# Batch 1's first FFN half prepared and begun before the first exponentials of batch 0's attention

## The chip, the cores and the metric

The kernel runs on one core of a Trainium2 chip. The metric is the device time of one execution in microseconds (us). Before the change it is 2087.34 us, the median of 3 runs (2084.44 to 2087.61).

## The reference

The input x is (4, 1024, 256) in float32: 4 batches of 1024 rows. Three steps follow one another, each added to x:

```python
x = x + 0.5 * ffn(layernorm(x))       # mixture of 8 experts, 2 chosen per row, and a shared one
x = x + attn_block(layernorm(x))      # 16 heads of 64, then an MLP of 256 -> 512 -> 256
x = x + 0.5 * ffn(layernorm(x))       # the same weights again
```

In the FFN a router (a 256 x 8 product, a sigmoid, the two largest scores, divided by their sum) gives each row a weight for every expert. Each expert is `gelu(x @ W1 + b1) @ W2 + b2` with 128 hidden values and the exact GELU. The shared expert has the same sizes and no weight. In the attention, scores are divided by 16 and a mask adds -999 to one corner element of the 1024 x 1024 scores (first query, last key); then softmax, values, output projection, and an MLP with the tanh form of GELU.

## The kernel before, in words

All large products are made of three float16 matmuls: each operand is split in a high and a low half (`mm3`, L952), and the products high-high, high-low and low-high are added in PSUM.

**Attention** runs over 32 pairs of heads (4 batches x 8 pairs), each in 4 units (2 heads x 2 halves of the queries), each unit in 4 steps: 512 steps, numbered i. Three things belong to a step. `maxima` (L1405) multiplies a block of 128 queries by all keys (two matmuls at L1425) into the PSUM tile S0, and DVE reduces it (L1432). After four of them a short chain, `row` (L1456), writes the negative maxima into the operand `low` by a DMA (L1467). `scores` (L1470) makes 2 x 512 transposed scores with the maxima already subtracted, four matmuls (L1489, L1490) into S1; ACT takes the exponential (line L550, in the helper `tabled`), ACT casts it to float16 (L1501), and POOL subtracts for the low half (L1504). `values` (L1525) multiplies by V. Maxima run LM = 6 steps ahead of scores.

**Jobs.** FFN and MLP work is done in halves of a batch (512 rows), each a `Job`. An FFN job (`ffn`, L1056) has `prep` (layer norm by `stats`, transposing by `transposed`, the router, and the loads of three gate rows `gb`), nine first layers (`layer`, L1101, six matmuls each at the helper line L948, then `rest`: GELU on ACT, times the gate on DVE at L1138, a cast on ACT at L1148, a subtraction on DVE at L1153), and four `second` parts (27 matmuls with W2 and one with the biases). The shared expert is number 8 and goes first in `ORDER`; it has no gate and one DVE step (L1151). Batch 0's two jobs (`fronts[0]`) run first, in `first_jobs` (L391), before attention; there the gate is made by a matmul (L1121) in one of four half tiles of S0 and S1, called places. All later jobs run between attention's steps.

**The order is planned by hand.** `Order` (L100) keeps a model clock for PE, ACT, DVE and POOL. Each piece of work is a generator, a chain with a rank, that yields `Ask`s: engine time, a PSUM bank (`BANK`; three F banks), an `ld` buffer (`LD`; two), a condition (`IF`), or a time to land (`DMA`). `until` (L269) waits in the model for the next step of attention and lets chains use PE meanwhile (`other`); `share` (L286) gives chains `SHARE` us of PE before and after each step's scores. `choose` (L217) lets a chain's operation go ahead of attention's own on an engine only if it ends at most a little late. Instructions of those four engines go to the chip in the planned order. SP, which issues all DMAs, is in order as well, but its order is not written out here.

GELU and the exponential use different ACT tables. `gelus` counts GELUs that are owed. While it is above zero, no exponential is planned: `exps` carries the condition

```python
self.then("ACT", 1.03, exps, 0, lambda: self.pt_live < BPT and self.order.gelus == 0)
```

`serve` (L429) takes the jobs after batch 0 in turn, and `prepare` (L381) runs the prep of the next one. In the kernel before, both wait until batch 0's two jobs are done entirely, and the nine layers of an FFN job are made together by `block` (L1626), which stops the exponentials, takes S0 and S1 too, and puts layer after layer on PE. A job starts only when the PE time given to jobs is below `target`, `RATE * (max(i, 0) + NEAR) + DONE`.

`attention` (L1574) starts with `ahead(14)`, which waits for `low_ready`, then for the first projections, and issues the first stack (`stack`, L1346: DMAs that lay Q and K of a head as `AC` and `low`). Seven maxima come before the first score.

Of the kernel before, what the change touches and what calls it, by code (L numbers as in the profile page):

```python
# [51 lines left out]
RANK, RREST = -2, -3  # L52
WAIT, AGE, LATE, LPOOL, SLOW = 2.0, 0.2, 1.6, 2.3, 0.7
SHARE, RATE, LEAD, NEAR, OWED = 0.7, 0.58, 40, 20, -16.0
BLD = 2
# [21 lines left out]
GBT, ROWT, MWT = 4.2, 3.2, 8.0  # L77
DONE = 23.4
NV = 3
LM = 6  # L80
# [225 lines left out]
class Kernel:  # L306
# [74 lines left out]
    def prepare(self):  # L381

        while True:
            yield Ask("IF", lambda: self.fronts[0][1].done and self.prep_ok and all(j.done for j in self.ends) and bool(self.jobs) and
                      not self.jobs[0].prepared and (self.jobs[0].dep is None or self.jobs[0].dep.done))
            job = self.jobs[0]
            for ask in job.prep:
                yield ask
            job.prepared = True

    def first_jobs(self):  # L391
# [4 lines left out]
        order.places = [(0.0, h) for h in self.halves]  # L396
        self.passed, self.exps = [False, False], 0

        def job(n, job):
# [14 lines left out]
            self.passed[n] = True  # L414
            yield Ask("IF", lambda: job.evicts == 0)
            order.start(self.ending(job), -8)

        self.setup()
        for n, j in enumerate((one, two)):
            order.start(job(n, j), -12 + n)  # L420

    def place_for(self, to):
# [6 lines left out]
    def serve(self, job, hp):  # L429

        yield Ask("IF", lambda: all(j.done for j in self.fronts[0]))
        while True:
            if job is None:
                yield Ask("IF", lambda: not self.closing and bool(self.jobs) and self.jobs[0].prepared and
                          self.order.done[3] < self.target)
                job = self.current = self.jobs.pop(0)
                self.prep_ok = False
                raw, hp = self.hidden(False)
                if job.pieces > 4:
                    self.block = job, hp  # L440
                    yield Ask("IF", lambda: self.block is None)
                else:
                    yield from job.burst(raw, hp)
                    yield Ask("IF", lambda: job.left == 0)
                self.prep_ok = True
# [513 lines left out]
    def router(self, xt, slot, half, spread):  # L959

        nc, wk = self.nc, self.mp
        n = 4
        own, at = spread and self.order is not None, []
        if own:
# [60 lines left out]
        elif not spread:  # L1025
            self.free()
            yield Ask("BANK")
            yield Ask("LD", 1)
        yield Ask("PE", 0.44)
# [21 lines left out]
        elif not spread:  # L1051
            self.free()
            self.free_ld()
        return gt

    def ffn(self, x, slot, half, burst, after, dep=None):  # L1056
# [44 lines left out]
        def layer(i, e, hp, ps, free=None):  # L1101
# [6 lines left out]
            def rest():  # L1108
                own, at = spread and self.order is not None, []
                if own and e < E:  # L1110
# [50 lines left out]
        def second(t, hp):  # L1161
            own, at = spread and self.order is not None, []
            if own:
# [87 lines left out]
    def front_h(self, b, half, x=None):  # L1251
# [12 lines left out]
        for t in range(4):  # L1264
            yield Ask("POOL", 0.56)
            nc.gpsimd.tensor_scalar(h[:, t, :], x[:, t, :], r[:, t, 0:1], nb[:, t, 0:1], ALU.mult, ALU.add)
        yield Ask("IF", lambda: self.bo_ready)
        for t in range(4):
# [305 lines left out]
    def attention(self):  # L1574
# [11 lines left out]
        def ahead(i):  # L1586
# [7 lines left out]
            if i == 14:  # L1594
                order.until(lambda: self.low_ready or None, 0)
            for lead, part in ((14, 0), (17, 1)):
# [66 lines left out]
        with self.tc.manual_schedule(engines={E_.PE, E_.Activation, E_.DVE, E_.Pool}):  # L1663
            self.first_jobs()
            order.start(self.serve(None, None), 3, 4.0)
            order.start(self.prepare(), 4)
            for i in range(-A, N + LVX):
                self.target = RATE * (max(i, 0) + NEAR) + DONE
# [219 lines left out]
```

## Time and profile before

| | us |
|---|---|
| median of 3 runs | 2087.34 |
| profiled execution, time | 2090.07 |
| its span | 2088.3 |
| first exponential starts | 140.3 |
| last exponential starts | 1931.2 |
| PE busy | 1975.2 |
| DVE busy | 1468.7 |
| ACT busy | 1496.9 |
| POOL busy | 1400.3 |

The span runs from the first to the last instruction of the profiled execution. Of it 140 us lie before the first exponential (weights split, batch 0's FFN, first projections), 1791 us are attention with the jobs between its steps, and 157 us are the last MLP and FFN halves. In the answers below, an instruction's line is followed by engine, operation, output <- input, shape and count, and in brackets by the idle time of its engine just before it and what ended that. SPq is the queue of DMA issues. Window rows give for each engine the busy us and, in brackets, the count.

### The profile page before, as it was taken

The numbers are of one execution on the slowest core, as the hardware profiler recorded it, in microseconds if no ns is written. First come the engines' busy times: TensorE is split into PE (matmuls) and PEld (weight loads), VectorE is DVE, ScalarE is ACT, GpSimd is POOL, SyncE is SP. The second block draws the span as 40 slices with busy tenths as digits, with TensorE's granted clock in tenths as the row PEclk, the third lists the DMA queues.
The fourth block names the chain that finished last, engine by engine and source line by source line (L and its number), as shares of the span: only waits on it lengthen the run. The fifth ranks groups of instructions, "written<-read, shape, count | busy, mean of one in ns | idle before, by whom it ended". The sixth has DMA issues, their size and how long they took to land.

```text
span 2088.3 us, 53062 instructions
## 1 busy us (share of the span) xinstructions
PE 1975.2 (95%) x22468; PEld 1287.9 (62%) x22468; DVE 1468.7 (70%) x2460; ACT 1496.9 (72%) x1785; POOL 1400.3 (67%) x891
## 2 busy tenths in 40 slices
PE   6979999999999999999999999999999999989789
PEld 3635666665666666657566666666665666656456
DVE  6567776766777777776777767677677576765654
ACT  6347768678777787778777768787778587777653
POOL 6654848577766987748577877777576788776300
PEclk9989999999999999999999999999999999999899
DMA  6532322434332423144324231333222414231100
GB/s 177 151 80 80 100 80 57 120 80 106 74 90 67 97 52 92 48 107 87 95 60 125 69 85 50 95 74 85 69 70 77 110 34 105 43 91 37 31 1 31
DMA packets 213020, 166.22 MB, mean 80 GB/s; under 512 B 140991, under 2 KB 172872, under 8 KB 212782
## 3 DMA queue, kind: packets, MB, share of 16 engines
q1 hardware_dynamic: 212782, 162.83, 30.9%
q8 instruction: 176, 2.88, 0.6%
q14 instruction: 62, 0.51, 0.1%
HBM read 70.18 MB, written 13.83 MB: 40 GB/s over the span
## 4 chain that ended last, share of the span: by engine, by line
PE 78%; ACT 5%; issue 3%; POOL 3%; DVE 2%; DMA 1%; POOLq 0%; ACTq 0%; DVEq 0%; SPq 0%
PE F L948 30%; PE S L1489 10%; PE S L1490 9%; PE S L1425 9%; PE av L1542 6%; PE av L1541 5%; PE av L1539 5%; POOL pk L1504 2%; ACT pt L550 2%; PE S L948 1%; ACT pk L1501 1%; ACT L550 1%; PE S L1459 1%; ACT ld L897 0%; DMA hp<-mwd 0%
## 5 line engine op out<-in xcount | busy, mean ns | idle before, releaser
L1504 POOL TENSOR_TENSOR pk<-pt,pk 128x1024 f16<-128x1024 f32 x512 | 1088.4, 2133 | 428.2 <-ACT pk L1501 208.2
L1432 DVE TENSOR_REDUCE mx<-S 128x1 f32<-128x1024 f32 x512 | 626.1, 1223 | 287.8 <-PE S L1425 262.0
L550 ACT ACTIVATE pt<-S 128x1024 f32<-128x1024 f32 x512 | 524.5, 1024 | 344.3 <-PE S L1490 321.0
L1501 ACT CAST pk<-pt 128x1024 f16<-128x1024 f32 x512 | 535.1, 1046 | 15.3
L1542 PE MATMUL av<-V,pk 128*128 128x65 f16 x4096 | 429.2, 193 | 16.9 <-POOL pk L1504 15.4
L1541 PE MATMUL av<-V,pk 128*128 128x64 f16 x4096 | 435.5, 195 | 0.0
L1539 PE MATMUL av<-V,pk 128*128 128x65 f16 x4096 | 434.6, 193 | 0.9 <-DVE at L1555 0.7
L1539 PEld LDWEIGHTS <-pk 128*128 128x128 f16 x4096 | 382.5, 97 | 54.4 <-issue 0.6
L1541 PEld LDWEIGHTS <-pk 128*128 128x128 f16 x4096 | 380.9, 97 | 53.9 <-issue 1.4
L1489 PE MATMUL S<-low 128*128 128x512 f16 x1024 | 389.6, 380 | 11.6 <-ACT pt L550 10.9
L1542 PEld LDWEIGHTS <-pk 128*128 128x128 f16 x4096 | 380.5, 99 | 22.3 <-POOL pk L1504 20.8
L1490 PE MATMUL S<-AC 128*128 128x512 f16 x1024 | 389.9, 381 | 0.0
L1425 PE MATMUL S<-AC 128*128 128x512 f16 x1024 | 307.6, 382 | 27.4 <-DVE mrow L1463 18.1
L948 PEld LDWEIGHTS <-hp 128*128 128x128 f16 x2100 | 206.1, 99 | 76.3 <-issue 9.3
L948 PE MATMUL F<-xA,wq 128*128 128x512 f16 x768 | 185.5, 379 | 1.1 <-DVE hp L1153 1.1
L948 PE MATMUL F<-wfs,hp 128*128 128x256 f16 x1404 | 180.4, 276 | 3.8 <-ACT u L550 2.8
L1490 PEld LDWEIGHTS <-AC 128*128 128x128 f16 x1024 | 100.1, 98 | 124.6 <-issue 37.3
L1489 PEld LDWEIGHTS <-low 128*128 128x128 f16 x1024 | 100.2, 98 | 106.4 <-issue 2.1
L948 PEld LDWEIGHTS <-wfs 128*128 128x128 f16 x864 | 84.1, 100 | 107.0 <-issue 17.6
L948 PEld LDWEIGHTS <-wq 128*128 128x128 f16 x768 | 74.3, 98 | 87.8 <-issue 1.9
L948 PE MATMUL F<-xF,wfs 128*128 128x512 f16 x504 | 122.9, 389 | 4.2 <-ACT u L550 2.8
L1425 PEld LDWEIGHTS <-AC 128*128 128x128 f16 x1024 | 75.4, 97 | 47.1 <-issue 33.5
(238 smaller groups left out, 2527.7 us busy)
## 6 DMA issues: line engine op xcount, KB each, us to landing
AC<-qk SPq DMA_DIRECT2D x128, 256.0 KB
gb<-gd SPq DMA_DIRECT2D x88, 256.0 KB
low<-qk SPq DMA_DIRECT2D x64, 256.0 KB
wq<-wqd SPq DMA_DIRECT2D x33, 384.0 KB
hp<-mwd SPq DMA_DIRECT2D x6, 1024.0 KB
x<-in_L_attn_x_dram SPq DMA_DIRECT2D x8, 512.0 KB
x1d<-x SPq DMA_DIRECT2D x8, 512.0 KB
wo<-wod SPq DMA_DIRECT2D x16, 256.0 KB
```

What stands on the lines that cost most here:

```text
L550: i = self.nc.scalar.activation(out, in_, func, **kw).ins
L948: i = self.nc.tensor.matmul(*args, start=start, **kw).ins
L1425: mm(ps[:, hs], AC[:, 0, qs], AC[:, 1, hs], start=True, stop=(h == 0 or t > 0), skip_group_check=True)
L1432: nc.vector.tensor_reduce(self.mx[:, t % 4:t % 4 + 1], ps, AX.X, ALU.max, negate=True)
L1459: nc.tensor.transpose(tp[:4, :P], mx[:], self.ident[:])
L1489: mm(o, low[:, 1, ks], low[:, 0, qs], start=True, stop=False, skip_group_check=True)
L1490: mm(o, AC[:, 1, ks], AC[:, 0, qs], start=False, stop=True, skip_group_check=True)
L1501: nc.scalar.copy(pk[:, 0], pt[:])
L1504: nc.gpsimd.tensor_tensor(pk[:, 1], pt[:], pk[:, 0], ALU.subtract)
L1539: mm(o[:, 0:65], pk[:, 0, ps], v[:, 0:65], start=(n == 0 and c == 0 and t == 0), stop=False, skip_group_check=True)
L1541: mm(o[:, 0:64], pk[:, 0, ps], v[:, 65:129], start=False, stop=False, skip_group_check=True)
L1542: mm(o[:, 0:65], pk[:, 1, ps], v[:, 0:65], start=False, stop=(n == 3 and c == 1), skip_group_check=True)
```

## The change

A new chain, `early_prep`, with rank `EARLY` = -6, runs the prep of batch 1's first half as soon as batch 0's first half has its `h` (`h_made`), that is while batch 0's second half runs. `prepare` starts after it (`early`), no longer after batch 0's jobs. `serve` starts when the last product of batch 0's second half is evicted (`over`). It makes the nine layers of its first job one by one in F banks, as chains that go where PE is free, and not as a block; GELUs are owed from that moment on. The router of that job uses places of S0 and S1 instead of F banks, and `ahead(14)` waits until it is through (`routed`). `SHARE` goes from 0.70 to 0.72.

```diff
-SHARE, RATE, LEAD, NEAR, OWED = 0.7, 0.58, 40, 20, -16.0
+SHARE, RATE, LEAD, NEAR, OWED = 0.72, 0.58, 40, 20, -16.0
+EARLY = -6
 def prepare(self):
-            yield Ask("IF", lambda: self.fronts[0][1].done and self.prep_ok and all(j.done for j in self.ends) and bool(self.jobs) and
+            yield Ask("IF", lambda: self.early and self.prep_ok and all(j.done for j in self.ends) and bool(self.jobs) and
...
 def first_jobs(self):
-        self.passed, self.exps = [False, False], 0
+        self.passed, self.exps, self.h_made, self.over = [False, False], 0, False, False
+        self.early = self.routed = False
...
             yield Ask("IF", lambda: job.evicts == 0)
+            self.over = n == 1
             order.start(self.ending(job), -8)
+    def early_prep(self):
+
+        yield Ask("IF", lambda: self.h_made)
+        for ask in self.jobs[0].prep:
+            yield ask
+        self.jobs[0].prepared = self.early = True
 def serve(self, job, hp):
-        yield Ask("IF", lambda: all(j.done for j in self.fronts[0]))
+        yield Ask("IF", lambda: self.over)
+        early = True
...
-                if job.pieces > 4:
+                if early:
+                    early = False
+                    self.order.gelus = len(ORDER)
+                    for i, e in enumerate(ORDER):
+                        yield Ask("BANK")
+                        yield Ask("PE", 1.3)
+                        u, rest = job.layer(i, e, hp, self.F_()[:], self.free)
+                        self.order.start(rest, RREST)
+                elif job.pieces > 4:
                     self.block = job, hp
 def router(self, xt, slot, half, spread):
-        own, at = spread and self.order is not None, []
+        own, at = self.order is not None and (slot == 0 or slot == 2 and half == 0), []
...
             self.free()
             yield Ask("BANK")
+        if not spread:
             yield Ask("LD", 1)
...
             self.free()
+        if not spread:
             self.free_ld()
+            self.routed = True
 def ffn(self, x, slot, half, burst, after, dep=None):
-                own, at = spread and self.order is not None, []
+                own, at = slot == 0, []
...
-            own, at = spread and self.order is not None, []
+            own, at = slot == 0, []
 def front_h(self, b, half, x=None):
+        self.h_made = True
         yield Ask("IF", lambda: self.bo_ready)
 def ahead(i):
             if i == 14:
-                order.until(lambda: self.low_ready or None, 0)
+                order.until(lambda: self.low_ready if self.low_ready and self.routed else None, 0)
 def attention(self):
             order.start(self.prepare(), 4)
+            order.start(self.early_prep(), EARLY)
```

## The prediction

> **What bounds the kernel now.** I read the page's slices first. TensorE (PE) is busy in nearly every slice from the third to the last ten per cent, so from about 150 us on work taken off PE shortens the run. Two places stand out, the first 7% and the tail after the last exponential (1931 us). The change touches the first, so I cut that by windows; columns are busy us (count) of PE, PEld, DVE, ACT, POOL, then clock, DMA share, GB/s.
>
> ```profile
> 102.50:123.00 20.50, 16.49 (x113) 9.23 (x110) 13.83 (x27) 3.13 (x6) 10.11 (x17) 0.92 0.34 84
> 123.00:140.25 17.25, 8.43 (x21) 2.49 (x22) 11.07 (x18) 4.60 (x7) 3.94 (x6) 0.59 0.65 160
> 178.69:196.68 17.99, 17.25 (x145) 9.78 (x144) 14.24 (x21) 12.14 (x18) 2.13 (x1) 1.00 0.29 98
> 140.25:1931.20 1790.95, 1738.40 (x20916) 1146.66 (x20915) 1290.62 (x2054) 1358.95 (x1547) 1294.55 (x752) 1.00 0.32 79
> ```
>
> From 123 to 140.25 us PE works 8.43 of 17.25 us, at a granted clock of 0.59. In the 1791 us of the steady part it is idle for 52.6 us, 3%. The PE timeline shows why it waits in the hole:
>
> ```profile
> 123.11 0.60 PE L1425 MATMUL S<-AC 128*128 128x512 f16 x2 [1.89 <-DMA AC<-qk]
> ...
> 125.53 0.59 PE L1425 MATMUL S<-AC 128*128 128x512 f16 x2 [1.76 <-DVE mx L1432]
> 127.44 1.01 PE L1425 MATMUL S<-AC 128*128 128x512 f16 x2 [1.32 <-DVE mx L1432]
> 129.77 1.01 PE L1425 MATMUL S<-AC 128*128 128x512 f16 x2 [1.31 <-DVE mx L1432]
> ...
> 137.50 1.01 PE L1425 MATMUL S<-AC 128*128 128x512 f16 x2 [1.31 <-DVE mx L1432]
> 138.30 0.63 PE L1489 MATMUL S<-low 128*128 128x512 f16 x1
> ```
>
> Each first maximum (two matmuls) waits for VectorE (DVE) to reduce the one before: one PSUM tile, one chain, nothing else ready. The reduction takes 1.22 us, and DVE waits about 1.10 us for the next. The ScalarE (ACT) timeline gives the rest:
>
> ```profile
> 133.35 1.28 ACT L550 ACT_TABLE_LOAD   x1
> 140.25 1.02 ACT L550 ACTIVATE pt<-S 128x1024 f32<-128x1024 f32 x1 [5.62 <-PE S L1490]
> ...
> 178.69 1.28 ACT L550 ACT_TABLE_LOAD   x1
> 180.37 0.66 ACT L550 ACTIVATE F<-F,b1f 128x512 f32<-128x512 f32 x1 [0.41 <-PE F L948]
> ...
> 194.48 0.66 ACT L550 ACTIVATE F<-F,b1f 128x512 f32<-128x512 f32 x1 [0.63 <-PE F L948]
> 195.39 1.28 ACT L550 ACT_TABLE_LOAD   x1 [0.24 <-PE S L1490]
> ```
>
> The first exponential is at 140.25. The nine layers of batch 1's first job run as a block between the table loads at 178.69 and 195.39, where PE is already full (17.25 of 17.99 us).
>
> **The change part by part.** I sum against the profiled execution, 2090.07 us (span 2088.3); the median shown is 2087.34, 2.7 lower, and the difference is applied to that.
>
> (A) *Nine layers leave the full stretch.* In the block six L948 matmuls start every 1.29 to 1.30 us (twelve from 182.97 to 185.56: 2.59). Nine layers are 9 x 1.295 = 11.7 us. In the new place they should lie in PE's holes, whose size I check under D. **-11.7**.
>
> (B) *The block's overhead.* PE is idle 0.74 us in it. The stretches from 176 to 198 and 198 to 215 lose 0.8 us each. Bounds 0 and -1.6; I take the block's own, **-0.7**. The two table loads there vanish, but PE did not wait for them.
>
> (C) *Router and gate transposes*: 24 small matmuls from 145.17 to 145.77, and four transposes (0.60 us in their row of the first job). They move to before the maxima: bounds 0 and -1.2, **-1.0**.
>
> (D) *The first exponential.* It needs all nine GELUs granted (`gelus == 0`), so the layers must be through first. Three F banks exist, and a layer's bank is held until its last DVE step; expert layers have two DVE steps (L1138 0.70, L1153 0.69), the shared one one. PE has room: at full clock a pair of maxima matmuls takes about 0.43 us against 1.22 on DVE, and a layer of 1.3 fits behind it. DVE is the narrow place. Of seven maxima (123.11 to 137.50) each leaves DVE a gap of about 1.1 us, room for one 0.7 us step: seven steps, 3.5 layers. Three more lie in the banks, so 6.5 layers are on PE by the first score at 138.3. The other 2.5 follow at the block's pace, (194.48 - 180.37) / 8 = 1.76 us, 4.4 us in all; then 0.66 for a GELU and 1.28 for the table load, which now has no idle time to lie in (the one at 133.35 had 5.62 us behind it). That is 144.6, 4.4 us late. I add 0.6 for sharing the queue with the gate loads: **+5**. Low end: every layer fits, and the fuller PE keeps its clock. Four maxima at 2.33 us spacing then go at 1.91 (the spacing at 125.53), -1.7, and the first two-block score takes 0.86 instead of 1.71, -0.85; with the table load +1.28, that is -1.3. High end: preparation comes so late that no layer starts before 137.5; nine at 1.76, a GELU and the load are 17.8, less the 2.75 us from there to the old exponential: +15.
>
> Why I believe the preparation arrives: batch 1's x is loaded at 79.03 already, since SP goes there as soon as the tile is free (L1205 after POOL h L1266). Its LayerNorm to router takes 22 us in the old place (123.14 to 145.17) and the gates 20 us more (165.0), beside a busy DVE. From 83 us this gives 105 and 125 at the old pace, less if ACT, idle from 88.5 to 107, answers sooner. The router's exponential can't go before the GELUs of job two are through (82.46), and costs a table load in that idle time; the GELU load after it too. So the change has as many switches as before; only the last is exposed.
>
> *A rule that speaks against it:* the Trainium skill, ScalarE: Activation LUTs, "What ACT_TABLE_LOAD costs", puts a switch at about 2.66 us, 1.28 for the load and 1.38 for a drain. The trace shows the load as 1.28 us and the next exponential 1.29 us after its start (195.39 to 196.68), so a drain could only lie ahead of it. By the page the exposed switch would cost 1.4 us more and the sum would be -6.5.
>
> (E) *Early preparation in the way of batch 0's end.* From 63 to 106 us PE is full, so DVE, ACT and POOL have slack there: nothing. From 102.47 to 113.19 the end of job two is one chain (stats on DVE, POOL, ACT, transposes on PE, projection). A router unit on DVE (1.3 us), a POOL subtraction (1.15) or two ACT scalings (1.09) can each stand ahead of a step of it. Bounds 0 and +3.5, the three together; **+0.5**, since most should be over by 102 or wait on DMA. Cover gone, it is the 3.5. On SP the move puts one x load, two transposes (2.71 us to issue), a 0.32 us store and three gate loads (1.28 together) before the stack loads; the last four are near the AC loads, which PE waits for (1.89), in a time of DMA share 0.65. That is the 0.6 in D, bounded by 0 and 3 (768 KB at the 236 GB/s of 120 to 130 us is 3.3). The new wait for `routed` gates only the issue of the stack, and other work is planned meanwhile; behind it are the first maxima, so a late router is priced in D's high end.
>
> (F) *SHARE 0.70 to 0.72, and a new order of everything after.* Two calls a step give 0.04 us more filler per step; total filler is the same. PE's waits from 145 to 1931 us are about 48 us in all (DVE mrow 17.3, POOL pk 15.4, ACT pt 10.7, small ones). A new order reshuffles these: I take **0**, bounds +5 and -5, a tenth of them.
>
> Sum: -11.7 - 0.7 - 1.0 + 5 + 0.5 = **-7.9**, so 2082.2 for the profiled execution and 2079.4 for the median; I say **2079 us**. Ends added: -20.8 and +11.8. What is late next in the hole is DVE, and in the steady part PE as before.
>
> **Rivals.**
> 1. *The first exponential pays it back* (no change): preparation ends near 132, layers at the block's pace reach 148 and the exponential is at 150, +10; with A to C and E net -3: about **2084**. For it: the old chain took 42 us to the gate store plus its loads. Against: DVE has no reductions before 123 and ACT is idle.
> 2. *The ninth GELU is late* (slower). DVE puts two steps into every period, 1.22 + 1.39 plus 0.5 of latency, 3.1 us a layer; begun at 132, nine end at 160, and the exponential with its load at 161.5, 21 us late. Net 21 - 13.4 = +8, **2095**. It decides from a first exponential at 157.9 (140.25 + 13.4 saved + 4.2). For it: the exponentials are shut from the moment the first layer is planned, and layers only go where PE idles. Against: after the score nothing competes for DVE but these layers.
> 3. *It doesn't do what it says*: not prepared before the maxima, the layers spread among the first steps, holes as before and a block less dense: **2087**.
>
> **How the numbers follow.** A measurement here can tell about 0.2% (4.2 us) from no change. Forecast (all of its spread from -4.2 down): 0.66. Rival 1: 0.13, same. Rival 2, with the bad end of F in it: 0.15, slower. Rival 3: 0.06, same. So faster 0.66, same 0.19, slower 0.15. The low end adds half of D's and F's good ends to the sum (2079.4 - 3.2 - 2.5 - 1), near 2072; below it I leave 0.1. The high end cuts rival 2 in its middle, 2092, leaving 0.1.
>
> **What would show it.** Right: L948 F<-xF,wfs matmuls between L1425 pairs before the first exponential; granted clock above 0.9 where it was 0.59; first exponential between 139 and 148; no table loads near 180; exponential number 33 about 8 us earlier than its 251.0 now. A step is wrong if the first exponential is after 150 (D), if job two's projection starts after 115 (E), or if the gain at exponential 33 is gone at 512 (F). The forecast is wrong if the steady part is held by something other than PE, so that a block less shortens nothing.

## The result, and the profile after

The changed kernel takes 2121.24 us (median of 4 runs, 2116.07 to 2125.08) against 2086.84 us of the kernel before (4 runs): a ratio of 1.0162, 95% interval 1.0149 to 1.0175. It is slower by 34 us. The profiled execution took 2116.07 us with a span of 2114.2.

Line numbers of the changed kernel are higher: the matmul helper is L967 (was L948), the maxima L1448 (L1425), their reduction L1455, scores L1512 and L1513, the exponential L569, the gate's product L1160, the second DVE step of a layer L1175. The windows of the changed kernel, cut at the first early layer and at the first and last exponential (us busy and count for PE, PEld, DVE, ACT, POOL, then clock, DMA share, GB/s):

```profile
102.50:118.83 16.33, 13.80 (x103) 6.94 (x100) 15.08 (x39) 4.93 (x10) 9.10 (x15) 1.00 0.32 91
118.83:152.29 33.46, 21.88 (x94) 9.05 (x95) 22.35 (x33) 12.80 (x20) 0.00 (x0) 0.90 0.46 122
152.29:1958.20 1805.91, 1728.64 (x20815) 1140.56 (x20813) 1276.14 (x2012) 1343.95 (x1523) 1293.77 (x752) 0.99 0.31 77
```

Three things are in these rows. The layers do lie in the hole: PE works 21.88 us there where it worked 8.43. But the hole has grown from 17.25 us (counted from the first maximum) to 33.46 us (counted from the first early layer), so PE is idle for 11.6 us in it, more than the 8.8 before. And from the first to the last exponential PE has 9.8 us less to do (1738.40 before) and yet the stretch is 15.0 us longer (1790.95 before): PE is idle for 77.3 us in it, not 52.6.

**The hole.** PE timeline of the changed kernel:

```profile
118.81 1.47 PE L967 MATMUL F<-xF,wfs 128*128 128x512 f16 x6 [0.26 <-DVE qk L1317]
...
125.76 1.46 PE L967 MATMUL F<-xF,wfs 128*128 128x512 f16 x6
132.37 1.01 PE L1448 MATMUL S<-AC 128*128 128x512 f16 x2 [5.15 <-DVE mx L1455]
...
135.29 2.72 PE L967 MATMUL F<-xF,wfs 128*128 128x512 f16 x6 [0.22 <-DVE hp L1175]
...
142.24 0.38 PE L1512 MATMUL S<-low 128*128 128x512 f16 x1
...
146.91 2.75 PE L967 MATMUL F<-xF,wfs 128*128 128x512 f16 x12 [0.33 <-DVE hp L1175]
```

Layers and maxima alternate as planned until 127 us. Then PE stands for 5.15 us, said to wait for DVE's maximum. DVE's own timeline says what DVE did meanwhile:

```profile
125.03 0.68 DVE L1173 SCALAR_TENSOR_TENSOR hp<-F,hp 128x512 f16<-128x512 f32 x1
131.02 0.17 DVE L647 TENSOR_SCALAR mb<-mb 128x4 f32<-128x4 f32 x1 [5.31 <-DMA mb<-mb1d]
131.09 1.22 DVE L1455 TENSOR_REDUCE mx<-S 128x1 f32<-128x1024 f32 x1
```

It did nothing. The maximum at 131.09 was ready long before, but ahead of it in DVE's order stood a step of 0.17 us, the scaling of the first MLP bias (`mb`, which only the MLPs read), and that waited for a DMA. SP's queue shows its two halves, the row's way out to memory and its way back as columns:

```profile
122.83 0.49 SPq L643 DMA_DIRECT2D mb1d<-gb  x1
...
128.02 0.43 SPq L593 DMA_DIRECT2D mb<-mb1d  x1
```

In the kernel before DVE made this row at 113.30, and the two issues are at 114.01 and 116.12, so that the columns had landed when DVE came to them at 124.22. Now DVE makes it at 118.67, after the early job's router and gates; the way out stands on SP behind the stack's loads until 122.83, the way back until the way out has landed, and DVE, which gets to it in its planned place, waits until 131.02. The DMA engines are full while the row goes out (share 1.05 between 122.83 and 128.02; 0.69 between 114.01 and 116.12 in the kernel before), so both the queue's order and the full engines can hold it, and no run tells the two apart. So the early work delays a bias, the bias holds DVE, DVE holds the maxima, and PE's granted clock falls (0.50 from 131.5 to 138 us): the six matmuls at 135.29 take 2.72 us, those at 125.76 took 1.46. ACT's timeline ends the hole:

```profile
118.83 1.28 ACT L569 ACT_TABLE_LOAD   x1 [5.14 <-DVE qk L1317]
...
150.31 0.67 ACT L569 ACTIVATE F<-F,b1f 128x512 f32<-128x512 f32 x1
150.99 1.28 ACT L569 ACT_TABLE_LOAD   x1
152.29 1.02 ACT L569 ACTIVATE pt<-S 128x1024 f32<-128x1024 f32 x1
```

The ninth GELU is at 150.31 and the table load is exposed, as predicted; the first exponential is at 152.29, 12.0 us later than before.

**The steady part.** The waits of PE by what ended them, in the whole run of the changed kernel (us in total, times, longest):

```profile
PE av L1565 <- POOL pk L1527: 24.8, 21, 7.3
PE F L967 <- DVE hp L1175: 14.8, 7, 5.3
PE S L1448 <- DVE mrow L1486: 14.4, 18, 0.9
...
PE S L1512 <- DMA low<-qk: 6.9, 1, 6.9
```

Before, the first was 15.4 us with a longest of 4.8, the second 1.8 with 0.8, and the last was not there. The new waits are few and long, and behind the longest of each of these three kinds stands a DMA. The 7.3 us for POOL are at 1667.7, where POOL itself stood 7.96 us for `h<-x1d`, which SP issued at 1666.92; this one is not new, for the kernel before has its 4.8 us at the same place (POOL stood 7.35 us for the same load). The others are new. PE timeline, two of them:

```profile
228.84 0.59 PE L1512 MATMUL S<-low 128*128 128x512 f16 x1 [6.88 <-DMA low<-qk]
...
1192.83 3.57 PE L967 MATMUL F<-xF,wfs 128*128 128x512 f16 x8 [5.00 <-DVE hp L1175]
```

The 6.88 us begin at 222 us, in step 24. SP's queue ahead of it:

```profile
209.75 5.23 SPq L1398 DMA_TRANSPOSE aT<-pk  x1
...
218.81 1.30 SPq L1112 DMA_DIRECT2D gb<-gd  x3
...
221.91 0.64 SPq L1383 DMA_DIRECT2D low<-qk  x1
```

The issue of a transposing DMA took 5.23 us, the gate loads of the second job came behind it, and the operand `low` that the next score needs (256 KB) came last, with the DMA engines full until it landed (share 1.01). Likewise at 1187.8 us: PE waits 5.00 us for a layer's DVE step, DVE for a gate, and SP had spent 5.30 us on a transpose at 1178.39 and 5.46 us on the gate loads at 1185.41. The two others end at 366.66 (5.28 us) and 596.89 (2.84 us), both for a layer's DVE step as well, with DVE waiting 3.92 and 3.10 us for a gate. These four and the 2.4 us more for POOL are 22.4 of the 24.7 us that PE is idle longer between the exponentials.

### The profile page after: what moved, and what is told of

Read it like the earlier page. It is cut to its first block, busy times and chain, and to the rows that moved or that the text cites. A ratio compares the mean times of both kernels' runs of the same rounds, so it can differ in the third digit from the quotient of the medians.

```text
span 2114.2 us, 53040 instructions
## 1 busy us (share of the span) xinstructions
PE 1976.7 (93%) x22468; PEld 1287.4 (61%) x22468; DVE 1470.4 (70%) x2460; ACT 1496.1 (71%) x1785; POOL 1399.4 (66%) x891
## 4 chain that ended last, share of the span: by engine, by line
PE 77%; ACT 6%; POOL 4%; issue 4%; DVE 4%; DMA 4%; SPq 0%; POOLq 0%; ACTq 0%; DVEq 0%
PE F L967 30%; PE S L1512 10%; PE S L1513 9%; PE S L1448 9%; PE av L1565 5%; PE av L1564 5%; PE av L1562 5%; POOL pk L1527 3%; PE S L967 2%; ACT pt L569 2%; DMA gb<-gd 1%; ACT pk L1524 1%; DVE S L1160 1%; ACT L569 1%; PE S L1482 1%
## 5 line engine op out<-in xcount | busy, mean ns | idle before, releaser
L1455 DVE TENSOR_REDUCE mx<-S 128x1 f32<-128x1024 f32 x512 | 626.2, 1223 | 311.6 <-PE S L1448 281.6
L569 ACT ACTIVATE pt<-S 128x1024 f32<-128x1024 f32 x512 | 524.1, 1024 | 369.1 <-PE S L1513 351.3
L1524 ACT CAST pk<-pt 128x1024 f16<-128x1024 f32 x512 | 535.1, 1046 | 15.7 <-DMA aT<-pk 0.3
L1512 PE MATMUL S<-low 128*128 128x512 f16 x1024 | 389.8, 381 | 20.0 <-ACT pt L569 10.9
L1513 PE MATMUL S<-AC 128*128 128x512 f16 x1024 | 389.3, 380 | 0.0
L1448 PE MATMUL S<-AC 128*128 128x512 f16 x1024 | 306.9, 381 | 22.7 <-DVE mrow L1486 14.4
L967 PEld LDWEIGHTS <-hp 128*128 128x128 f16 x2100 | 205.4, 98 | 77.0 <-issue 9.1
L967 PE MATMUL F<-xA,wq 128*128 128x512 f16 x768 | 187.8, 381 | 1.5 <-DVE qk L1317 0.9
L967 PE MATMUL F<-wfs,hp 128*128 128x256 f16 x1404 | 178.2, 274 | 4.7 <-ACT u L569 2.8
L1513 PEld LDWEIGHTS <-AC 128*128 128x128 f16 x1024 | 100.2, 98 | 122.7 <-issue 35.9
L1512 PEld LDWEIGHTS <-low 128*128 128x128 f16 x1024 | 100.3, 98 | 114.9 <-DMA low<-qk 7.3
L967 PEld LDWEIGHTS <-wfs 128*128 128x128 f16 x864 | 84.7, 100 | 122.8 <-issue 21.4
L967 PE MATMUL F<-xF,wfs 128*128 128x512 f16 x522 | 130.2, 394 | 18.5 <-DVE hp L1175 14.8
L967 PEld LDWEIGHTS <-wq 128*128 128x128 f16 x768 | 74.1, 98 | 88.1 <-issue 2.4
L1448 PEld LDWEIGHTS <-AC 128*128 128x128 f16 x1024 | 74.7, 97 | 41.9 <-issue 29.7
```

Source lines behind the costliest of these rows:

```text
L569: i = self.nc.scalar.activation(out, in_, func, **kw).ins
L967: i = self.nc.tensor.matmul(*args, start=start, **kw).ins
L1448: mm(ps[:, hs], AC[:, 0, qs], AC[:, 1, hs], start=True, stop=(h == 0 or t > 0), skip_group_check=True)
L1455: nc.vector.tensor_reduce(self.mx[:, t % 4:t % 4 + 1], ps, AX.X, ALU.max, negate=True)
L1512: mm(o, low[:, 1, ks], low[:, 0, qs], start=True, stop=False, skip_group_check=True)
L1513: mm(o, AC[:, 1, ks], AC[:, 0, qs], start=False, stop=True, skip_group_check=True)
```

## The experiments

**Theory one**, after these readings: the early work does what it should; the loss is the order that the planner makes of everything behind it (the second job starts on step 25 instead of 45, as soon as it is prepared), with SHARE as a part. **Theory two**: the early work has a price of its own, by the late first exponential and by buffers and queues taken early.

To read the runs I cut each profiled execution at exponentials 0, 80 and 511 (counted from 0, as the steps are) and compare with the kernel before: 140.3 us to the first, 299.3 from 0 to 80, 1491.6 from 80 to 511, 157.1 behind, 2088.3 in all. The table gives differences to these in us; medians and ratios are of all runs. A row of differences is one execution, and executions of one kernel lie up to 12 us apart (e13: 2088.8 to 2098.7, and the profiled one is its slowest), so that the columns are read for what is large. The first exponential alone varies by some 4 us: up to it e10, e14 and e18 run the same instructions in the same order on PE, DVE, ACT and POOL, and it is at 150.0, 145.5 and 145.9. Where the third job starts on another step, the two middle columns exchange a few us.

| kernel | first exp. | 0 to 80 | 80 to 511 | behind | span | median | ratio (95%) |
|---|---|---|---|---|---|---|---|
| changed | +12.0 | -6.4 | +21.5 | -1.1 | +26.0 | 2121.2 | 1.0162 (1.0149 to 1.0175) |
| e1 SHARE 0.70 | +14.8 | -9.1 | +20.5 | -3.9 | +22.2 | 2115.0 | 1.0142 (1.0124 to 1.0160) |
| e3 late bias | +11.1 | -6.7 | +24.0 | -3.2 | +25.2 | 2111.0 | 1.0116 (1.0098 to 1.0133) |
| e4 block, early | +14.7 | -15.7 | +18.8 | -1.2 | +16.6 | 2110.8 | 1.0123 (1.0102 to 1.0143) |
| e7 gate loads from ACT | +15.6 | -12.0 | +20.2 | -0.9 | +22.9 | 2117.2 | 1.0147 (1.0131 to 1.0162) |
| e12 job two held to 32 | +16.9 | -9.5 | +9.5 | -2.4 | +14.6 | 2104.5 | 1.0075 (1.0059 to 1.0091) |
| e17 prep two held to 14 | +16.3 | -18.1 | +22.9 | -0.9 | +20.2 | 2113.3 | 1.0128 (1.0112 to 1.0143) |
| e5 0.70, job two at 46 | +15.6 | -21.4 | +18.4 | -3.4 | +9.1 | 2098.3 | 1.0060 (1.0044 to 1.0077) |
| e9 0.70, all jobs held | +18.1 | -12.8 | -0.5 | -2.8 | +2.0 | 2093.8 | 1.0027 (1.0017 to 1.0038) |
| e10 e9 and late bias | +9.7 | -12.9 | +3.1 | -3.2 | -3.2 | 2085.7 | 0.9992 (0.9981 to 1.0003) |
| e13 0.70, job two at 45 | +18.2 | -12.0 | +2.1 | +0.3 | +8.6 | 2093.3 | 1.0029 (1.0016 to 1.0043) |
| e14 e13 and late bias | +5.3 | -11.9 | +1.2 | +0.6 | -4.9 | 2088.1 | 1.0002 (0.9991 to 1.0012) |
| e15 e13, layers not early | +3.1 | +2.7 | +3.4 | -2.5 | +6.7 | 2093.1 | 1.0025 (1.0013 to 1.0036) |
| e18 e14, not pinned | +5.6 | -10.0 | +2.4 | -1.8 | -3.7 | 2090.0 | 1.0012 (1.0004 to 1.0021) |
| before, e2 SHARE 0.72 | -2.8 | -4.2 | +13.5 | -0.1 | +6.3 | 2097.5 | 1.0057 (1.0042 to 1.0072) |
| before, e6 SHARE 0.71 | -4.4 | -6.1 | +24.0 | -1.0 | +12.5 | 2103.3 | 1.0082 (1.0066 to 1.0098) |
| before, e11 SHARE 0.69 | -3.3 | -1.5 | +25.9 | -1.1 | +20.0 | 2109.4 | 1.0101 (1.0086 to 1.0116) |
| before, e8 jobs moved | -2.5 | -21.8 | +38.9 | -2.9 | +11.6 | 2101.6 | 1.0083 (1.0065 to 1.0102) |
| before, e16 job two at 46 | -3.3 | -2.0 | +25.5 | -3.5 | +16.7 | 2105.4 | 1.0086 (1.0071 to 1.0100) |

**e1**: SHARE back to 0.70 in the changed kernel; **e2**: SHARE 0.72 in the kernel before; **e6**: 0.71 in the kernel before.

```diff
-SHARE, RATE, LEAD, NEAR, OWED = 0.72, 0.58, 40, 20, -16.0
+SHARE, RATE, LEAD, NEAR, OWED = 0.7, 0.58, 40, 20, -16.0
```

> The changed kernel with SHARE back at 0.70. Theory 1 (the loss comes from waits that the new order makes: 5.2 us on VectorE at 126 us, and about 17 us more of waits on single DMAs from 220 us on, wherever the jobs fall on the 16-step cycle of a pair): the first exponential stays at 152, and the rest moves by some 10 us either way, since the order is new again, between 2100 and 2130. Theory 2 (SHARE 0.72 costs the drift of some 20 us from exponential 200 on): 2095 to 2103, with exponential 176 still about 8 us late and no further drift.

> The kernel before with SHARE 0.72 alone. Theory 2: 2100 to 2110, with the drift after exponential 200. Theory 1: the first exponential at 140 as before, and the rest within some 10 us of 2087, 2080 to 2100, depending on the waits that this order meets.

> The kernel before with SHARE 0.71: nothing but another order of the same work. If the order before is a lucky one among many, this one is 5 to 20 us slower, 2092 to 2107, as with 0.72. If an order is worth no more than 5 us: 2082 to 2092.

Taking SHARE back brings 6.3 us of the 34 by the medians, though the two intervals overlap. Giving it to the kernel before costs 12 us, and 0.71, half the step, costs 17. So this number has no direction in which it is better: each value deals the same work into another order, and the two new orders are both worse by far more than the 5 us that the prediction allowed a new order.

**e3**: the scaling of `mb` is planned 14 us later, so that DVE doesn't meet its DMA among the first maxima. **e7**: the gate rows are loaded from ACT's queue instead of SP's.

```diff
-        yield Ask("DMA", 6.0)
+        yield Ask("DMA", 20.0 if name == "mb1" else 6.0)
```
```diff
-QG = 'sync'
+QG = 'scalar'
```

> The changed kernel, but the scaling of the MLP's bias (VectorE, 0.17 us) is planned 14 us later, so that VectorE does not stand 5.3 us on its DMA among the first maxima. Theory 1: the first exponential at 147 to 148 instead of 152, and the whole about 5 us less, 2111 to 2121, if the rest of the order stayed; it is new as well, so plus or minus 8. Rival (VectorE's own work sets the first exponential): it stays at 151 to 153.

> The changed kernel, its gate rows loaded from ScalarE's queue and not SP's, so that they neither wait behind other DMAs there nor hold them up. If SP's order makes the waits at 127, 222, 361, 594 and 1188 us: those shrink and the kernel is 10 to 20 us faster than the changed one, 2101 to 2111. If they come from DMA traffic or from ScalarE's place in the order: 2115 to 2130, with ScalarE waiting for VectorE where it issues.

In e3 the wait is gone: the third reduction starts 1.9 us after the second, where it started 7.2 us after. But the first reduction came 3.8 us later in this run (125.80 for 121.98), so that the first exponential is at 151.4, not at the 147 to 148 that the same start would have given. The median is 10 us under the changed kernel's. e7 is 4 us under the changed kernel, with intervals that overlap. With no gate load on SP the bias still comes back late (issued at 128.95, scaled at 132.85 after a last wait of 0.15 us for the DMA), so that the gate loads ahead of it are not what holds it; and now ACT, in order too, stands behind a gate load until 129.00, with the first GELU's table load (129.39) behind it, and DVE stands 5.88 us for ACT. Of the later waits that it was made for, those at 222 and 361 us shrink to 4.62 and 1.73 us, the one at 594 goes, and 4.97 us in two are left near 1188. The column from 0 to 80 is 5.6 us better for it than the changed kernel's, but the first exponential is 3.5 us later, and 80 to 511 is still 20.2 us longer.

**e4**: the preparation is early, but the nine layers are made as a block in one piece, still ahead of the first exponential (`early = False` in `serve`).

> The changed kernel, with the early preparation, but the first job's nine layers made as a block like all later ones, before the first maxima or among them. If one by one between the maxima is what costs: first exponential before 150. If the early work itself is too much for the time there: first exponential at 150 or later. Steady part as open as in the others; total 2090 to 2125.

It is 10 us under the changed kernel, though its first exponential is 2.7 us later. That layers go one by one is not what makes the first exponential late, and 24 of the 34 us stay without it.

**e8** asks whether the steps alone do it: in the kernel before, jobs two to four may not start ahead of steps 57, 87 and 120, where the changed kernel has its third to fifth. The means is a condition in `serve` that later runs use too (`HOLDP` does the same to the preparation, in `prepare`):

```diff
+HOLD, HOLDP = {1: 57, 2: 87, 3: 120}, {}
...
-                          self.order.done[3] < self.target)
+                          self.order.done[3] < self.target and self.at >= HOLD.get(self.begun, -99))
```

> The kernel before, its second, third and fourth jobs held until steps 57, 87 and 120, the steps of the changed kernel. Theory 1: it takes over some of the changed kernel's waits, the 5 us at step 57 and 3 us at 120, and is 5 to 20 us slower than before: 2092 to 2107. Rival (steps don't matter): 2083 to 2090.

No wait of PE over 1.5 us turns up at these steps, so that a block on them is not bad in itself. The order behind is: 80 to 511 is 38.9 us longer (part of that is work put off from the column before), and a kernel with nothing of the change in it is 15 us slower.

**e5**: the changed kernel, SHARE 0.70, with the second job's preparation held to step 14 and its layers to 46.

```diff
+HOLD, HOLDP = {1: 46}, {0: 14}
```

> The changed kernel with SHARE 0.70, and with the second job held: its preparation waits for step 14 and its layers for step 46, where the kernel before has them. The first job stays early. Theory 1 (the early part gains, and what is lost comes later, from the steps at which the following jobs fall): after exponential 48 this kernel runs like the one before, 3 to 8 us ahead of it: 2078 to 2086. Rival (the early work or its prolonged DMAs cost by themselves, wherever the later jobs lie): above 2095.

2098.3: 23 us of the 34 are gone by SHARE and by holding one job. At exponential 448 the run is 12.2 us ahead of the kernel before, part of it by work put off; then exponentials 448 to 464 take 81.8 us, 53.3 in the kernel before, with PE idle for 13.1 of them, 0.1 before. That jump comes back in several of the other orders: 82.7 in e1, 89.9 in e6, 91.1 in e8, 83.8 in e11, 82.1 in e16. It is not in all: the changed kernel, e3, e4, e7 and e17 take 55.3 us there, e2, e9, e10 and e12 61 to 62. So the changed kernel loses elsewhere, and a new order can lose in more than one way.

**e12**: the changed kernel with only the second job held to step 32.

```diff
+HOLD, HOLDP = {1: 32}, {}
```

> The changed kernel (SHARE 0.72) with only the second job's layers held until step 32 instead of 25. Theory one: the 6.88 us for which TensorE stood at 222 us, with VectorE's scores waiting on a small DMA that stood on SP's queue behind the second job's loads, is gone, and the time falls by 7 to 10 us, to 2105 to 2115 us. Rival: such a wait turns up at another place or the planner's later deal takes the gain back: 2116 to 2125 us.

The time went where it was expected and a little further (2104.5), but not for the reason given: the wait at step 24 is still there, 7.37 us at 226.8. It belongs to the second job's preparation, whose gate loads are issued there, not to its layers. What went is 12 us from exponential 80 on: again an order that is another one.

**e9** and **e10**: SHARE 0.70 and every later job held to about the steps of the kernel before; e10 with the late bias as well.

```diff
+HOLD = dict(enumerate((46, 74, 104, 133, 152, 183, 218, 246, 279, 309, 338, 378, 406, 429, 455, 499), 1))
+HOLDP = {0: 14}
```

> The changed kernel with SHARE back at 0.70 and every later job (the second onward) held to the step at which the kernel before starts it (46, 74, 104, 133 and so on), so that only the first job differs in order. Theory one: the early work itself is worth what stands at exponential 16 (about 3 us to the mean of the kernels without it, 8 us to the kernel before), and the rest of the loss is the order that the planner makes behind it; with the order of before pinned, the time is 2078 to 2086 us, and the lead over the kernel before at exponential 16 is still there at exponential 208 to within 4 us. Rival: the early work itself (first exponential 12 us late, buffers taken early) costs later on, whatever the order: 2095 us or more, with the loss spread over exponentials 16 to 208.

> The kernel of the run before (SHARE 0.70, all later jobs held to the steps of before) with the late scaling of the first layer's bias as well, so that VectorE does not stand 5.3 us between the second and third maximum. Theory one: first exponential some 4 us earlier than in the run before and the time 0 to 4 us under it, 2074 to 2086 us. Rival: the wait moves to the DMA of the added gate behind it and the time is that of the run before.

e9 lies between the two theories: 27 us of the 34 go with the order and SHARE, but 6.4 stay by the medians, and the profile puts them at the first exponential (18.1 us late). e10 takes 8 us more away by the late bias and has the lowest median of all; against the kernel before it is not told from no change (0.9981 to 1.0003).

**e11**: the kernel before with SHARE 0.69.

> The kernel before with SHARE 0.69 in place of 0.70: no early work, only a planner that deals the same work in another order. Theory one (the order of the kernel before is an exceptionally good one, and any other deal costs what 0.71 and 0.72 cost): 2092 to 2107 us. Rival (time falls steadily with a smaller share, so that 0.72 alone explains the loss): 2082 to 2090 us.

Slower by 22 us. On both sides of 0.70 the order is worse; the kernel before has a better one than any of its neighbours that were tried.

**e16** makes that as small as it can be: the kernel before, its second job not ahead of step 46. By itself the planner puts it on 45.

```diff
+HOLD, HOLDP = {1: 46}, {}
```

> The kernel before with one number more: its second job may not start ahead of step 46, where it starts at 45 by itself. Nothing of the change is in it. The planner then puts the later jobs on 74, 105, 126, 166, 201, 247 up to 505. Theory one (the order of the kernel before is an exceptionally good one and a step's shift of one job loses it): 2096 to 2108 us. Rival (a shift by one step costs about that step, and the losses above are the early work's): 2085 to 2091 us.

One step, nothing else, and 17.7 us are lost. In the two traces PE runs the same instructions in the same order up to exponential 45 and another order from there. The largest part of the loss lies in one place: of 22.9 us that PE is idle longer between the exponentials, 13.9 are between 448 and 464, and 9.5 between 80 and 208. Windows from exponential 448 to 464, first of e16, then of the kernel before:

```profile
1715.42:1797.54 82.12, 68.09 (x738) 44.54 (x735) 49.60 (x75) 47.05 (x56) 56.63 (x45) 0.92 0.39 96
```
```profile
1720.35:1773.63 53.28, 53.21 (x666) 36.75 (x663) 36.44 (x50) 38.67 (x43) 45.67 (x25) 1.00 0.43 103
```

In the kernel before PE is never idle there; in e16 it is idle for 14 us, at a lower clock, with 15 us more work pushed into these steps. PE's timeline of e16 names the two largest waits (L1547 is the values' product, L953 the helper):

```profile
1728.36 0.23 PE L1547 MATMUL av<-V,pk 128*128 128x65 f16 x1 [7.29 <-POOL pk L1509]
...
1749.22 0.81 PE L953 MATMUL F<-hp 128*128 128x256 f16 x6 [3.76 <-DVE hp L1792]
```

Values wait 7.29 us for POOL, and an MLP's second product waits for DVE with no other work to put in.

**e13** is the same question from the other side: e5 with 45 in place of 46.

```diff
-HOLD, HOLDP = {1: 46}, {0: 14}
+HOLD, HOLDP = {1: 45}, {0: 14}
```

> The kernel of the run in which the second job was held to step 46 (SHARE 0.70, its preparation held to step 14), with 45 in place of 46: one number. In the planner's output every later job then starts on the step at which the kernel before starts it (73, 103, 133, 152 up to 499), where 46 gave 70, 99, 127, 166 up to 505. Theory one (the loss is the order that the planner makes behind the early work, not the early work): the loss at exponential 448 to 464 and the 16 us of the run with 46 are gone, 2078 to 2086 us, and the lead or lag against the kernel before at exponential 16 is carried to the last exponential within 3 us. Rival (the early work has a price of its own that comes up late, whatever the order): 2092 to 2100 us.

With 45 the planner gives every later job the step that it has in the kernel before, unasked. The traces show more: from exponential 80 to 511, PE, DVE, ACT and POOL each run the same sequence of instructions in e13 as in the kernel before (in e14, e15 and e18 too), and in the changed kernel another. The windows from exponential 80 to 511, of the kernel before, of e13 and of the changed kernel:

```profile
439.61:1931.20 1491.59, 1448.45 (x17548) 958.32 (x17545) 1071.12 (x1681) 1138.93 (x1296) 1102.98 (x642) 1.00 0.32 79
```
```profile
445.82:1939.48 1493.66, 1448.87 (x17550) 958.35 (x17548) 1071.42 (x1681) 1138.56 (x1295) 1102.83 (x642) 1.00 0.32 79
```
```profile
445.20:1958.20 1513.00, 1452.41 (x17537) 959.16 (x17534) 1073.54 (x1665) 1136.46 (x1291) 1100.53 (x641) 0.99 0.32 78
```

PE's work in this stretch is nearly the same in all three (4 us more in the changed kernel, at a clock of 0.99). e13 takes 2.1 us more than the kernel before, the changed kernel 21.4, and none of the changed kernel's four new waits, of which two lie in this stretch, is in e13. So 19 of the 26 us between the spans arise here, nearly 300 us and more after the early work was done, and they go with the order. The time itself, 2093.3, is the rival's number: 5.6 us stay by the medians, 8.6 in the profile, and there they are, added up, the first exponential at 158.5 (+18.2; DVE stood 6.74 us for `mb` in this run) less 12.0 us won up to exponential 80, and 2.4 lost after it. The lead over the kernel before was not simply kept from exponential 16 on, either: all of the 12 us are won by exponential 16 (48.9 us from the first, 60.8 before), and from 16 to 80 the two take the same 238 us, though PE has 5.7 us less to do in e13 (226.5 for 232.2). It is idle for 11.9 us there, 6.3 before, in many waits of about a us and less, most for POOL and DVE.

**e14**: e13 with the late bias.

> The run before with the late scaling of the first layer's bias as well. Theory one: VectorE's stand of 5 us between the second and third maximum goes, the first exponential comes about 5 us earlier than in the run before, and so does the end: 2074 to 2083 us, under the kernel before. Rival: the wait moves to another DMA, and the time is that of the run before to within 2 us.

5.3 us under e13, so the rival of a moved wait falls; but at 2088.1 it is level with the kernel before, not under it. Its hole is the one that the prediction drew. PE timeline of e14 (L972 is the helper, L1453 the maxima, L1517 the scores):

```profile
127.15 0.59 PE L1453 MATMUL S<-AC 128*128 128x512 f16 x2
...
135.76 1.46 PE L972 MATMUL F<-xF,wfs 128*128 128x512 f16 x6
139.46 1.45 PE L972 MATMUL F<-xF,wfs 128*128 128x512 f16 x6 [2.25 <-DVE hp L1180]
140.75 0.38 PE L1517 MATMUL S<-low 128*128 128x512 f16 x1
...
142.04 1.46 PE L972 MATMUL F<-xF,wfs 128*128 128x512 f16 x6
```

Eight layers are through at the first score, and the first exponential is at 145.5. PE works 19.86 of the 26.68 us from 118.83 on, at full clock. This is an early one: in e10 and e3, which run the same instructions up to there, the first exponential is at 150.0 and 151.4, and their first maxima start at 125.56 and 125.11, where e14's starts at 121.38.

**e15**: e13 with the first job's layers back on step 14 as a block, only its preparation early.

```diff
-HOLD, HOLDP = {1: 45}, {0: 14}
+HOLD, HOLDP = {0: 14, 1: 45}, {0: 14}
...
-        early = True
+        early = False
```

> The early preparation alone, without the early layers: SHARE 0.70, the first job held to step 14 and made there as a block as in the kernel before, the second held to 45, so that all jobs start as in the kernel before. If the nine layers that leave the full stretch bring about 12 us and the late first exponential takes about as much back, this run has its first exponential at 136 to 141 us and a time within 4 us of the run with both: 2080 to 2087 us. If the early layers are worth what was predicted (11.7 less 5), it is 6 us or more above the run with both. If they cost more than they bring, it is under it.

The median is e13's within 0.3 us, so the layers bring as much as the late first exponential takes back; but the time is above the 2080 to 2087 expected. The table shows the exchange: without the early layers, 0 to 80 is 14.7 us longer, and the first exponential 15.1 us earlier. With the wait for the bias in it, the first exponential pays back all that the layers bring. And the early preparation alone costs 5.3 us against the kernel before; its first exponential is 5.8 us later than the mean of 137.5 in the six profiles of the kernel before's start. DVE's timeline of e15 has the wait for the bias in it as well, with no early layer there:

```profile
133.83 0.17 DVE L652 TENSOR_SCALAR mb<-mb 128x4 f32<-128x4 f32 x1 [3.59 <-DMA mb<-mb1d]
```

So the wait comes from the preparation, not from the layers. PE also waits 4.10 us for the first `AC` load in e15, 1.89 before; how much of the 5.3 us each of these is was not taken apart.

**e17**: the changed kernel, SHARE 0.72, with only `HOLDP = {0: 14}`; **e18**: e14 with `HOLD` empty, so that the second job starts on 41 and the rest as before.

> The changed kernel (SHARE 0.72) with one wait more in the planner: the second job's preparation may not start ahead of step 14. Its jobs then start on 40, 66, 94, 121 and from there within a step of the changed kernel (162, 194, 233, 264 up to 499). Theory one, two parts of the lost order: the early burst of the second to fourth jobs, with SP's queue held at 209.75 us and the 6.88 us that TensorE then waits at 222 us, is worth about 13 us by exponential 32 and goes; what the changed kernel loses behind exponential 208 (some 15 us more than the kernel before) stays. That is 2103 to 2110 us. Rival (the early burst is paid back later, and the loss is all in the later part): 2115 to 2122 us.

> The candidate: SHARE 0.70, the late scaling of the first layer's bias, and the second job's preparation not ahead of step 14, with no step pinned. The second job then starts on 41 and the third on 73, and all later ones on the steps of the kernel before. The two kernels with 45 lost some 8 us of their lead between exponentials 16 and 80 to short waits for POOL and VectorE, part of them while TensorE had no other work ahead of step 45. If starting at 41 saves a part of that: 2082 to 2087 us. Rival: the same time as the run with 45, 2088 us to within 2, or more if the order of the first 80 steps costs anew.

In e17 the wait of 6.88 us is gone and 8.0 us with it, less than expected; the 22.9 us from exponential 80 on stay. The early burst is the smaller part of the order's loss. e18 is no better than e14 (2090.0): four steps earlier for one job costs what it brings. No kernel here beats the kernel before by more than can be measured.

## Why the prediction was wrong

The forecast was 2079, the range to 2092; it is 2121. By its steps:

- **A to C** (layers, overhead and router leave the full stretch, -13.4) came out near their sum. Exponentials 0 to 80 are 11.9 to 12.9 us shorter in e9, e10, e13 and e14, where the later jobs are on about the steps of before; e15, without the early layers, has +2.7. That it is so near is in part chance, for it is the net of two things: in e14 PE has 16.0 us less to do there and is idle for 4.1 us more, and the prediction has no term for the second.
- **D** (first exponential +5, ends -1.3 and +15) had the right mechanism and missed a wait. 6 layers were on PE at the first score (6.5 were predicted), but that score came at 142.24, not 138.3, and the last layers took 8.1 us to the ninth GELU instead of 4.4. With the wait, the first exponential is at 152.3 in the profile shown and at 155 to 158.5 in e1, e5, e9, e12, e13 and e17, at and beyond the high end; the mean of the seven is 156.2. With the wait taken away it is at 145.5 and 145.9 in e14 and e18, for 145.2 predicted, but that match is luck: in e10 and e3 it is at 150.0 and 151.4, and the mean of the four is 148.2. Against 137.5, the mean of six profiles with the start of the kernel before, the first exponential is thus some 19 us late with the wait and 11 without it, where 5 was predicted. The term that failed first is the 0.6 "for sharing the queue with the gate loads": bytes and issue time were priced, while the cost was a chain that the prediction doesn't name, the bias row pushed back by 5.4 us on DVE and by SP's queue, with DVE's reductions behind it. It had no wait in the trace of before, only 8.1 us between the issue at 116.12 and its use at 124.22, landing included, and what the early work would do to them was not asked. Of the other 6 us, some 3 are there when the first maximum starts (123.4 in the mean of the four, 120.2 of the six); the rest was not taken apart.
- **E** (+0.5, ends 0 and 3.5) was right for what it names: job two's projection is at 108.4 for 113.19, no later. The bias row, which shares those engines, was not named, and e15 puts the price of the early preparation alone at 5.3 us, where C and E together say -0.5.
- **F** (SHARE and the new order, 0, ends -5 and +5) is the step that failed most. In the changed kernel the stretch from exponential 80 is 21.5 us longer. By medians, holding the order to that of before (e13, with SHARE 0.70) takes 27.9 of the 34.4 us away, and in the kernel before one step's shift of one job costs 17.7, SHARE 0.69, 0.71 and 0.72 cost 22, 17 and 12. "A tenth of PE's waits" took the 48 us of the kernel before for a typical sum that would be dealt anew. It was the low end: the other orders have more (in all of the stretch between the exponentials 64.7 us in e2, 68.0 in e8, 75.8 in e11, 77.3 in the changed kernel, for 52.6). All five disturbed orders of the kernel before are slower, by 12 to 22 us, so for this order the ends should have been 0 and some 25. Why it is so much better than its neighbours the runs don't show; that it was picked by its time would fit.
- **Rival 2** came nearest for the early work alone: it gave 2095 for a first exponential past 157.9, and e13 and e9, with 158.5 and 158.3, have 2093.3 and 2093.8. Its reason, two DVE steps in every period, is not what the trace shows. The rest of the loss was no rival at all.

Of the signs named, the layers between the maxima and the missing table loads near 180 came true, the clock in the hole is 0.90, and the first exponential after 150, exponential 33 (counted from 1, as the prediction does) not earlier but at 275.6 for 251.0, with one job more done by then, and the lag of 27.0 us at the last exponential each told the failure.

**What stays open.** In e14 the prediction's sum is left without its failed terms, and the profile has -4.9 us where -7.9 was predicted; the medians have +0.4. Part of this lies in the profile of before: its first exponential at 140.3 is later than in the five other profiles that share its start (135.8 to 137.7), so that "+5" was counted from a late one. With 11 in place of 5 the sum is about -2, near the +0.4 of the medians. The rest, the small waits between exponentials 16 and 80, was not taken apart. Whether the bias row is late by its place in the queue or by full DMA engines is open too. Nor was it tried to find an order for the early work by search. What makes e5 and e16 lose at 448 to 464 is seen (PE without other work, behind POOL), and so are the changed kernel's four new waits (for `low` and for gate rows), but not which decision of the planner leads there.

## What to carry to other kernels

In a kernel whose order is planned greedily, an edit at the start is two edits: itself, and a new order for all that follows; price the second by perturbing the kernel before (one step, one constant), and expect a loss where the old order is better than all its neighbours. To see what an edit itself is worth, pin the order behind it: here one number, 45 for 46, did it. When work is moved ahead on in-order engines and queues, look for what it pushes back that had slack and no wait, small constants too: they show no price in the old trace.

## What was not expected of the hardware

- The same order repeats almost to the tenth of a us: between exponentials 80 and 272 the difference of e13 to the kernel before goes from 6.2 to 6.5 us, over 668 us. Runs of one kernel differ by more (2082.56 to 2093.71 in 25 runs of the kernel before), and some of that lies ahead of this stretch: the first exponential alone was at 135.8 to 140.3 in six profiles with the same start.
- A wait of 5.15 us of PE was followed by matmuls at 0.54 of their rate (2.72 us for six, 1.46 before) at a granted clock of 0.50, so that it cost more than its length.
- A table load just ahead of the first exponential costs its 1.28 us and no more: it starts as the last GELU ends (150.31 and 0.67 long), at 150.99, and the exponential starts at 152.29.
